# A selective scan laid out over (state, channel of a group of eight) in place of one state at a time

## The chip, the cores and the metric

The kernel runs on one core of one Trainium2 chip. A core has five engines that each work through a queue of their own, in order: TensorE (PE, matrix products into PSUM), VectorE (DVE, elementwise work, reductions, scans), ScalarE (ACT, functions such as exp, copies), GpSimd (POOL, elementwise work on SBUF) and SyncE (SP, issues transfers). Time is microseconds of device time for the whole program. The kernel before took 25469.25 us, the median of three runs (25460.89, 25469.25 and 25479.85).

## The reference

The input is eight images of 64 channels and 64 x 64 positions. Four layers follow one another: attention over all positions with a depthwise block (layer 0), two blocks of attention in windows with an MLP (layer 1), filters made from the data with a 1 x 9 convolution (layer 2), and a selective scan in four directions followed by a small multi-scale block (layer 3). The change touches the scan of layer 3. Cut to that, for one image, 128 channels, 16 states, four directions k and 4096 positions in the order of the direction:

```python
x_dbl = einsum('bkdl,kcd->bkcl', xs, xproj_w)          # 4 + 16 + 16 rows
dts, Bs, Cs = split(x_dbl, [4, 20], axis=2)
dts = softplus(einsum('bkrl,kdr->bkdl', dts, dtproj_w) + dtproj_b)
A = -exp(A_logs).reshape(4, 128, 16)
def step(h, inp):                                       # over the 4096 positions
    u_t, dt_t, B_t, C_t = inp
    h = h * exp(dt_t[..., None] * A) + dt_t[..., None] * B_t[:, :, None, :] * u_t[..., None]
    return (h, einsum('bkcn,bkn->bkc', h, C_t))         # sum over the 16 states
```

So for every position there are 128 x 16 running states; each needs a decay factor exp(dt * A), an input dt * u * B, one step of the recurrence, and a product with C that is summed over the states. The four directions are added.

## The kernel before, in words

The images are handled in pairs; a tile's partitions are (image, channel). Layers 0 to 2 work on a pair. Layer 3 runs `ss2d` once for each image of the pair, with the 128 scan channels on the partitions, so there are eight scan stages in a run. Everything else of the program (layers 0 to 2, the norms, `safm`) is the same before and after the change but for one number, the slots of the pool of large tiles.

A scan stage goes through 16 units of work: four directions (0, 2, 1, 3), each cut into four pieces of `TC` = 1024 positions. For a piece, `scan_inputs` (from L777) makes what the scan needs: a matmul with 36 output rows (`px`, L787) gives B, C and the low-rank part of dt; the 32 rows of B and C are written to memory (`rows`, issued by ACT); a second matmul (`pd`, L803), absolute value, exp and log (L808 to L812) and two VectorE operations (L810, L813) give dt, and one more (L814) gives dt * u. These inputs are made for the piece after the one being scanned (`ahead`).

`scan` (from L819) then loops over the 16 states, partition = channel:

- `bc` (L842): a transfer of 1 MB, issued by SP, that copies the state's rows of B and C onto all 128 partitions.
- `da` (L844): ACT computes exp(dt * A[:, n]) with the state's column of A as the scale.
- `v` (L846): VectorE multiplies dt * u with B.
- `h` (L849): VectorE's scan instruction runs the recurrence along 1024 positions, from a carried column.
- `carry` (L852): ACT copies the last column out.
- `v` (L853): VectorE multiplies h with C.
- `y` (L837): PE adds v into PSUM with an identity matrix, two matmuls of 512 columns; it accumulates over the 16 states.

At the end VectorE adds y to the output `Y` (L861 or L863). Pools have two buffers for each name unless a number stands with them, so a step can run at most two states ahead of what consumes it. A scheduler fixes the order of instructions on each engine when the program is built; it places an instruction by the program's order and by when a buffer is free, and nothing is reordered when it runs.

## Time and profile before

| what | us |
| --- | --- |
| median of three runs | 25469.25 |
| the profiled execution, first to last instruction (its span) | 25403.5 |
| PE busy in it | 19006.6 |
| VectorE busy | 16255.3 |
| ScalarE busy | 6244.3 |
| GpSimd busy | 654.9 |
| the eight scan stages, first `px` to last addition to `Y` | 1408.4 to 1414.0 each |

The profile times every instruction of one execution. "Busy" is the time in which an engine had an instruction under way. A matmul of fp32 data appears as two records, each with a weight load of its own. In a group's line the count, the busy time, the mean of one instruction in ns, and the idle time of the engine ahead of the group are given, with what ended that idle time. PEclk is the share of TensorE's clock that was granted.

### The profile page before, as it was taken

To read this page: it belongs to the slowest core of one execution; us is meant where nothing else is said; L and a number is where in the kernel's file an instruction comes from. 1 tells how busy PE (TensorE), PEld (TensorE's weight loads), DVE (VectorE), ACT (ScalarE), POOL (GpSimd) and SP (SyncE) were. 2 spreads that over 40 slices of the span, in tenths; PEclk is the share of its full clock that TensorE was granted. 3 is DMA by queue.
4 is the path that set the end of the run, shared out by engine and by line. 5 is a ranking of instruction groups with operands and counts; after the bars stand their busy time and mean duration, and the time that the engine had idled before them with its cause. 6 is when DMAs were issued, how large, how long until landed. Compare 5 with 4: busy or idle time off the path is not lost.

```text
span 25403.5 us, 118768 instructions
## 1 busy us (share of the span) xinstructions
PE 19006.6 (75%) x41752; PEld 7027.5 (28%) x41752; DVE 16255.3 (64%) x13458; ACT 6244.3 (25%) x8413; POOL 654.9 (3%) x817
## 2 busy tenths in 40 slices
PE   9998855565999885555599888555659988856565
PEld 4433311111443331111144333111114433311111
DVE  2225589898222558989822255898982225589898
ACT  0123232232012323223201232322320123232232
POOL 0001000000000100000000010000000001000000
PEclk9787777777678777777767877777766787777776
DMA  0000045454000005545400000554540000055453
GB/s 14 2 0 1 1 170 193 155 195 144 7 2 0 1 1 172 194 156 195 142 5 2 0 1 1 176 193 154 195 142 5 2 0 1 1 176 193 156 196 136
DMA packets 570550, 2209.23 MB, mean 87 GB/s; under 512 B 35680, under 2 KB 35680, under 8 KB 568288
## 3 DMA queue, kind: packets, MB, share of 16 engines
q1 hardware_dynamic: 563520, 2181.17, 24.9%
q10 hardware_dynamic: 6432, 20.47, 0.3%
q8 instruction: 329, 5.39, 0.1%
q14 instruction: 269, 2.20, 0.0%
HBM read 2176.33 MB, written 25.17 MB: 87 GB/s over the span
## 4 chain that ended last, share of the span: by engine, by line
PE 47%; DVE 32%; DMA 17%; ACT 3%; issue 2%; DVEq 0%; ACTq 0%; POOL 0%
DMA bc<-rows 17%; PE s L366 14%; DVE h L849 11%; PE s L397 7%; PE po L390 7%; DVE v L846 5%; DVE v L853 5%; PE ws L510 3%; DVE n_sd L313 3%; PE av L546 2%; PE n_v L310 2%; PE pb L678 2%; PE pt L538 1%; PE py L690 1%; PE wpv L524 1%
## 5 line engine op out<-in xcount | busy, mean ns | idle before, releaser
L837 PE MATMUL y<-v,pack 128*128 128x512 f32 x8192 | 6098.2, 887 | 4265.7 <-DVE v L853 4265.7
L837 PEld LDWEIGHTS y<-v,pack 128*128 128x128 f32 x8192 | 1926.1, 259 | 8458.3 <-DVE v L853 6521.2
L849 DVE TENSOR_TENSOR_SCAN h<-da,carry,v 128x1024 f32<-128x1024 f32 x1536 | 3609.7, 2350 | 144.6 <-DVE v L846 4.6
L366 PE MATMUL s<-X 64*128 64x512 f32 x4096 | 3498.5, 1057 | 10.6 <-DMA X<-in_x 10.6
L844 ACT ACTIVATE da<-dt,A 128x1024 f32<-128x1024 f32 x2048 | 2327.8, 1137 | 1880.4 <-DVE h L849 1878.8
L846 DVE TENSOR_TENSOR v<-dtu,bc 128x1024 f32<-128x1024 f32 x2048 | 2503.5, 1222 | 433.6 <-DMA bc<-rows 411.8
L369 DVE TENSOR_REDUCE mx<-s 128x1 f32<-128x1024 f32 x1024 | 1253.5, 1224 | 2310.8 <-PE s L366 2310.8
L853 DVE TENSOR_TENSOR v<-h,bc 128x1024 f32<-128x1024 f32 x2048 | 2506.6, 1224 | 61.8
L407 DVE RECIPROCAL rec<-po 64x512 f32<-64x512 f32 x64 | 214.7, 3355 | 3378.1 <-PE po L390 3378.1
L366 PEld LDWEIGHTS s<-X 64*128 64x128 f32 x4096 | 1365.5, 334 | 2130.4 <-issue 2118.3
L397 PE MATMUL s<-RQ,QK 65*128 65x512 f32 x4096 | 1924.2, 593 | 0.0
L390 PE MATMUL po<-e,VT 128*128 128x512 f32 x4096 | 1917.8, 592 | 0.0
L852 ACT ACTIVATE carry<-h 128x1 f32<-128x1 f32 x1536 | 311.5, 203 | 5562.4 <-DVE h L849 5555.6
L401 ACT ACTIVATE e<-s 128x1024 f32<-128x1024 f32 x1024 | 1047.7, 1023 | 2441.8 <-PE s L397 2441.8
L313 DVE RECIPROCAL n_sd<-n_sd 128x512 f32<-128x512 f32 x288 | 963.1, 3348 | 588.1 <-ACT n_sd L312 588.1
L849 DVE TENSOR_TENSOR_SCAN h<-da,v 128x1024 f32<-128x1024 f32 x512 | 1172.9, 2291 | 46.7 <-DVE v L846 1.8
L510 PE MATMUL ws<-kx,Q 64*64 64x512 f32 x2048 | 1083.5, 722 | 8.4 <-DVE we L513 6.1
L390 PEld LDWEIGHTS po<-e,VT 128*128 128x128 f32 x4096 | 774.3, 189 | 982.5 <-issue 948.3
L397 PEld LDWEIGHTS s<-RQ,QK 65*128 65x128 f32 x4096 | 773.4, 189 | 976.5 <-issue 976.5
L379 ACT ACTIVATE RQ<-pm 1x512 f32<-1x512 f32 x64 | 37.6, 587 | 3550.2 <-PE pm L376 3549.9
L310 PE MATMUL n_v<-n_sq,pack 128*128 128x512 f32 x576 | 503.7, 971 | 428.5 <-DVE H L321 255.8
L787 PE MATMUL px<-XC,pack 128*36 128x512 f32 x512 | 424.6, 970 | 530.8 <-ACT XC L733 334.6
(207 smaller groups left out, 14412.4 us busy)
## 6 DMA issues: line engine op xcount, KB each, us to landing
bc<-rows SPq DMA_DIRECT2D x2048, 1024.0 KB, 5.2
rows<-xd ACTq DMA_DIRECT2D x128, 128.0 KB, 2.1
X<-in_x SPq DMA_DIRECT2D x4, 2048.0 KB, 10.3
QK<-in_x SPq DMA_DIRECT2D x8, 1024.0 KB, 7.2
RQ<-in_x SPq DMA_DIRECT2D x8, 1024.0 KB, 7.2
out<-Y SPq DMA_DIRECT2D x32, 256.0 KB, 2.0
pack<-in_w ACTq DMA_DIRECT2D x1, 3169.0 KB, 29.4
pack<-in_w ACTq DMA_DIRECT2D x1, 424.5 KB, 10.0
```

Source lines behind the costliest of these rows:

```text
L313: nc.vector.reciprocal(sd, sd)
L366: nc.tensor.matmul(s[:, h, :], lhsT=X[lo, t * P : (t + 1) * P], rhs=X[lo, o : o + CH], start=True, stop=True)
L369: nc.vector.tensor_reduce(mx[:, t, q : q + 1], s, AX.XY, ALU.max)
L390: nc.tensor.matmul(po, lhsT=VT[:, t, :], rhs=e[:, h, :], start=(t == 0), stop=(t == 31))
L397: nc.tensor.matmul(s[:, h, :], lhsT=QK[0:65, t * P : (t + 1) * P], rhs=RQ[0:65, cols], start=True, stop=True)
L401: nc.scalar.activation(e, s, AF.Exp, scale=C**-0.5)
L510: nc.tensor.matmul(s[lo], lhsT=Q[lo, cols], rhs=kx[lo], start=True, stop=True)
L837: nc.tensor.matmul(y[:, hc], lhsT=w["ident"], rhs=v[:, hc], start=(n == 0), stop=(n == NST - 1))
L844: nc.scalar.activation(da, dt, AF.Exp, scale=self.A[:, k, n : n + 1])
L846: nc.vector.tensor_tensor(v, dtu, bc[:, 0, :], ALU.mult)
L849: nc.vector.tensor_tensor_scan(along(h), along(da), along(v), first, ALU.mult, ALU.add)
L853: nc.vector.tensor_tensor(v, h, bc[:, 1, :], ALU.mult)
```

## The change

The scan is laid out anew. `TC` goes from 1024 to 512, so a stage has 32 pieces in place of 16. A step `u` of the inner loop no longer covers one state of 128 channels; it covers all 16 states of a group of eight channels, partition = state * 8 + channel. There are again 16 steps a piece. `r` is the strip of 32 channels that the group lies in, `q` its place in the strip.

- Decay: PE multiplies dt (the 32 channels of a strip, so 32 rows of contraction) with `asel`, a table that picks the eight channels and carries A; the product goes to PSUM (`da`, three buffers) and ACT applies exp in place there.
- Input: dt * u is written to memory (`rows`), and one transfer of 1 MB for each four steps (`ub`) brings each channel's row to its 16 partitions. B comes from a matmul whose weights repeat each state's row eight times (`BB`). GpSimd multiplies `ub` with `BB` into `v` (four buffers).
- Scan: VectorE, 512 columns, decay from PSUM and input from SBUF, result in `h` (three buffers).
- Product with C: on even steps GpSimd multiplies h with `CC` (SBUF), on odd steps VectorE multiplies h with `pc3` (the same values, made by one more matmul and kept in PSUM). Both write into `v`.
- Sum over states: PE multiplies v with `ysel`, which adds the 16 states of each of the eight channels into the strip's 32 rows of `y`; 128 rows of contraction, 32 output rows.
- `scan_inputs`: the low-rank product for dt is folded into one matrix beforehand (`xdt`), so one matmul gives `pd`; two more give `BB` and `CC`.
- The pool of large tiles has five slots in place of six, and the tables `asel` and `xdt` are made once at the start. The packed weights are larger.

Comments in the file went too; they are left out here.

```diff
-TC = 1024
+GD = P // NST
+TC = 512
 ...
-    put("xpT", np.concatenate([xp[:, RNK:], xp[:, :RNK]], axis=1).transpose(2, 0, 1))
 ...
+    put("xbT", np.repeat(xp[:, RNK : RNK + NST], GD, axis=1).transpose(2, 0, 1))
+    put("xcT", np.repeat(xp[:, RNK + NST :], GD, axis=1).transpose(2, 0, 1))
+    put("xr", xp[:, :RNK].transpose(1, 0, 2))
+    put("dtT", f["dtproj_w"].transpose(2, 0, 1))
+    e32 = np.eye(32, dtype=np.float32)
+    put("gsel", np.concatenate([e32] * 4, axis=0).reshape(P, 4, GD))
+    put("ysel", np.concatenate([e32.reshape(4, GD, 32)] * NST, axis=1).transpose(1, 0, 2))
 ...
-        self.slabs = ctx.enter_context(tc.tile_pool(name="slabs", bufs=6))
+        self.slabs = ctx.enter_context(tc.tile_pool(name="slabs", bufs=5))
 ...
+        self.asel = const.tile([P, KDIR, 4, NST * GD], F32, name="asel", tag="asel")
+        for k in range(KDIR):
+            for q in range(4):
+                nc.vector.tensor_tensor(
+                    self.asel[:, k, q].rearrange("p (n d) -> p n d", d=GD),
+                    A[:, k, :].unsqueeze(2).to_broadcast([P, NST, GD]),
+                    w["gsel"][:, q, :].unsqueeze(1).to_broadcast([P, NST, GD]),
+                    ALU.mult,
+                )
 ...
+            pd = ps.tile([P, CH], F32, name="pd", tag="pr", bufs=2)
+            nc.tensor.matmul(pd, lhsT=self.xdt[:, k, :], rhs=xc[:, h * nr : (h + 1) * nr, :], start=True, stop=True)
 ...
-        return rows, dt, dtu
+        rows = self.dram.tile([32, 4, TC], F32, name="rows", tag="rows")
+        nc.scalar.dma_start(rows.rearrange("m r t -> r m t"), dtu)
+        for to, wt in ((BB, "xbT"), (CC, "xcT")):
+            for h in range(TC // CH):
+                pb = ps.tile([P, CH], F32, name="pb3", tag="pr", bufs=2)
+                nc.tensor.matmul(pb, lhsT=w[wt][:, k, :], rhs=xc[:, h * nr : (h + 1) * nr, :], start=True, stop=True)
+                nc.scalar.activation(to[:, h * CH : (h + 1) * CH], pb, AF.Copy)
+        return rows, dt, BB, CC
 ...
+        pc = ps.tile([P, TC], F32, name="pc3", tag="pc", bufs=1)
 ...
+        for u in range(NST):
+            q, r = u // 4, u % 4
+            g = 4 * r + q
+            rs = slice(32 * r, 32 * r + 32)
+            if r == 0:
+                ubs = wk.tile([P, 4, TC], F32, name="ub", tag="ub")
+                nc.sync.dma_start(
+                    ubs.rearrange("p r t -> p (r t)"),
+                    rows[GD * q : GD * q + GD].rearrange("d r t -> d (r t)").unsqueeze(0).to_broadcast([NST, GD, 4 * TC]),
+                )
+            ub = ubs[:, r, :]
+            da = ps.tile([P, TC], F32, name="da", tag="da", bufs=3)
             for h in range(TC // CH):
                 hc = slice(h * CH, (h + 1) * CH)
-                nc.tensor.matmul(y[:, hc], lhsT=w["ident"], rhs=v[:, hc], start=(n == 0), stop=(n == NST - 1))
+                nc.tensor.matmul(da[:, hc], lhsT=self.asel[rs, k, q, :], rhs=dt[rs, hc], start=True, stop=True)
+            nc.scalar.activation(da, da, AF.Exp)
+            v = wk.tile([P, TC], F32, name="v", tag="v", bufs=4)
+            nc.gpsimd.tensor_tensor(v, ub, BB, ALU.mult)
+            h3 = wk.tile([P, TC], F32, name="h", tag="h", bufs=3)
+            first = 0.0 if at == 0 else self.carry[:, g : g + 1]
+            nc.vector.tensor_tensor_scan(along(h3), along(da), along(v), first, ALU.mult, ALU.add)
             if at < NTC - 1:
 ...
+            if u % 2:
+                nc.vector.tensor_tensor(v, h3, pc, ALU.mult)
+            else:
+                nc.gpsimd.tensor_tensor(v, h3, CC, ALU.mult)
+            for h in range(TC // CH):
+                hc = slice(h * CH, (h + 1) * CH)
+                nc.tensor.matmul(y[rs, hc], lhsT=w["ysel"][:, q, :], rhs=v[:, hc], start=(q == 0), stop=(q == 3))
+            if u == NST // 2:
                 following = ahead()
```

## The prediction

> **What bounds the kernel now.** I read the page's busy times and chain, then the windows of the scan stages, then the groups of the scan's lines, and last the rows elsewhere that resemble what the change adds.

> ```profile
> 3248.00:4657.00 1409.00, 839.44 (x1153) 256.86 (x1153) 1300.47 (x832) 423.22 (x546) 0.00 (x0) 0.75 0.56 192
> 4773.00:6185.00 1412.00, 848.56 (x1152) 261.81 (x1152) 1300.07 (x832) 422.80 (x546) 0.67 (x12) 0.74 0.56 193
> ```

> These are two scan stages: length, busy PE, weight loads, VectorE, ScalarE, GpSimd, granted PE clock, DMA share. VectorE works 1300 of 1409 us, GpSimd nothing. The eight stages are 11296 us by their first and last instructions, 44% of the span. Cut to pieces of 512 columns, as the change has them, a stage is 32 x 43.3 us and about 25 us at its ends, and VectorE's work is 40.6 us a piece.

> ```profile
> L849 DVE TENSOR_TENSOR_SCAN h<-da,carry,v 128x1024 f32<-128x1024 f32 x1536 | 3609.7, 2350 | 144.6 <-DVE v L846 4.6
> L846 DVE TENSOR_TENSOR v<-dtu,bc 128x1024 f32<-128x1024 f32 x2048 | 2503.5, 1222 | 433.6 <-DMA bc<-rows 411.8
> L853 DVE TENSOR_TENSOR v<-h,bc 128x1024 f32<-128x1024 f32 x2048 | 2506.6, 1224 | 61.8
> ```

> A step is 1222 + 2350 + 1224 ns of VectorE in a row, with little idle time, and what there is waits for the transfer of B and C. So the stage is worth what VectorE is relieved of, as long as no other engine takes its place.

> **The change part by part**, for a piece of 512 columns; there are 256.

> VectorE. Two rows at 512 and 1024 columns (681 ns at L683, 1224 at L853) leave a fixed part of 2 x 681 - 1224 = 138 ns. A scan of 512 is then (2350 + 138) / 2 = 1.25 us; bounds 1.18 (half) and 1.31 (two fixed parts). 16 scans are 20.0 us, 8 products with C at 0.68 are 5.4, `pd` 0.75 (L724 at 512), the softplus sum 0.68, dt * u (1565 + 138) / 2 = 0.85, the addition to Y (1965 + 138) / 2 = 1.05. Together 28.7 us against 40.6.

> GpSimd. The nearest row is a product of the same shape:

> ```profile
> L501 POOL TENSOR_TENSOR kx<-K,pack x512: 1037/1045/1167, 1988.3 to 21810.8; 128x512 f32<-128x512 f32 x171
> ```

> (min, median, max in ns.) 16 inputs and 8 products with C are 24 x 1.045 = 25.1 us, below VectorE's 28.7. [...]

> Do the two engines hinder each other?

> ```profile
> L516 DVE TENSOR_TENSOR we<-we,wmx x512: 678/692/1367, 2007.8 to 21824.2; 128x512 f32<-128x512 f32 x171
> ```

> ```profile
> L513 DVE TENSOR_TENSOR we<-ws,wbias x256: 631/680/693, 2487.7 to 21822.3; 128x512 f32<-128x512 f32 x128
> ```

> L516 reads two SBUF tensors and is stretched up to twice; matching times, those beside a `kx` average 844 ns, the others 687. L513 has one operand in PSUM: 680 beside a `kx`, 676 without. The new scans read decay from PSUM and the odd products C from PSUM, so I take no cost for them; the bound is 24 x 0.16 = 3.8 us a piece.

> ScalarE. 16 exps at 0.60 (L540, 128x512 from PSUM), 14 copies of 0.20, five more of 0.6 to 0.69, two table loads of 1.28: about 18 us. It doesn't bound.

> DMA. Four transfers of 1 MB a piece; the same size lands in 5.2 us (`bc`). The program's order gives each at least six GpSimd instructions, 6.3 us, after its buffer comes free, and `rows` is written a whole piece ahead. Cost nothing; if that cover went, up to 4 x 5.2 = 21 us a piece would show.

> PE. 36 matmuls of 512 columns a piece (16 decay, 16 sums, `pd`, `BB`, `CC`, `pc3`), two records each. A record takes 0.43 us at full clock and 0.86 at half, so 31.0 us or 61.6. This is the part to fear:

> ```profile
> 1000.00:1300.00 300.00, 300.00 (x353) 117.12 (x352) 107.35 (x89) 0.00 (x0) 0.00 (x0) 0.50 0.00 0
> 1500.00:1690.00 190.00, 190.00 (x444) 83.75 (x443) 12.15 (x6) 57.03 (x56) 0.00 (x0) 1.00 0.00 0
> ```

> Both windows of layer 0 have PE busy throughout. The first has only matmuls of 64 rows of contraction (L366) and stays at clock 0.50; the second has 65 and 128 rows and gets 1.00. The clock records change on a grid of 3.41 us. I summed, for each step of the grid, PE's streaming time weighted with rows / 128 (rounded up to 32). At half clock, a step under 0.70 was followed by full clock in 1% of 2598 cases, over 0.78 in 96% of 824. At full clock, a step under 0.39 kept it in 1% of 942, over 0.47 in 99% of 2122. Output columns didn't matter.

> The decay matmuls have 32 rows (weight 0.25), the sums 128. At full clock a piece streams 20 x 0.86 + 16 x 0.86 x 0.25 = 20.6 us, 0.59 of 35 us: it keeps the clock. At half clock and busy throughout, the mean is 24 / 36 = 0.67, too little, but the order has runs of 128-row matmuls (sums 5 and 6, `BB` or `CC`, sum 7; sum 11 with `pd`) that fill a step, so it returns within a piece. [...]

> Matmuls in different row strips overlap:

> ```profile
> 2389.68 1.44 PE L599 MATMUL ph<-H,pack 64*128 64x512 f32 x4
> ```

> Four records, partly at half clock, in 1.44 us. Where two decays or two sums stand together and are ready, they share a slot; the order has 27 slots for 36. A decay and a sum can't share.

> **Stalls.** I walked the order of one piece through the four queues. (a) Exp 9 stands behind the state copy of scan 8 on ScalarE: scan 9 starts 0.20 + 0.60 + 0.1 = 0.9 us late. (b) The table loads ahead of the next piece's first exp: 0.5. (c) `v` has four buffers; inputs 12 and 14 stand on GpSimd right behind products 8 and 10 and need their sums done first, so GpSimd idles 1.2 us twice (a sum takes 1.07 us to its end), and scans 13 to 15 wait: 1.3. (d) PE, 31.0 us of work in about 31, queues up, and a lapse of the clock for one step delays two matmuls by 0.86 each; from 0 (pairs, no lapse) up to a PE bound at half clock; I take two lapses a piece, 3.5 us, since 0.59 lies nearer to the full clock's rows. Total 28.7 + 0.9 + 0.5 + 1.3 + 3.5 = 34.9 us.

> Elsewhere: tables at the start and the larger weights, about 20 us, ahead of the first reductions on VectorE. The fifth slot: outside the scan the order is the same to a few instructions, and the tiles freed late are awaited by loads that 447 us of L366 cover. Nothing.

> **Sum.** 8 x (32 x 34.9 + 25) = 9134 against 11296: -2162, +20. The profiled execution is 25403.5; the median lies 65.75 above, and I keep that: 25469.25 - 2142 = 23327, say 23330.

> **The rivals.**
> 1. The clock stays low (the other side). For it: L366, 447 us at half clock, and the stage's mean of 0.75 now. Against: the 128-row runs. Then 27 to 36 slots at 1.71 us are 46.2 to 61.6 us a piece: 26200 to 30100. It decides above 43.3 us a piece, a mean slot of 1.20 us over 36.
> 2. GpSimd paces. Each even product waits for its scan (1.25) and the next input for the sum (1.2): with six of eight exposed 25.1 + 6 x 2.45 = 39.8 us, with eight 44.7; from 38 to 44.7 it gives 24100 to 25850, mostly still faster. For it: one queue with both kinds of work. Against: the order has two to four inputs ahead of most products.
> 3. VectorE and GpSimd block each other after all: 34.9 + 3.8 = 38.7 us, 24300; a full block of each of 24 by 0.69 gives 51.5, 27600. L513 speaks against it.

> **How the numbers follow.** Forecast 0.56, rival 1 0.16, rival 2 0.20, rival 3 0.08. Its own range is 22150 (scans at 1.18 us, term d at 0) to 24100 (38 us a piece). The range for 8 in 10 takes in rival 2 but for its end: 22150 to 25600, leaving out rival 1's 0.14, half of rival 3 and 0.02 below. Faster: 0.56 + 0.15 + 0.02 + 0.03 = 0.76; slower 0.22; same 0.02. Within 0.2% is about what a measurement can't tell from no change.

> **What would show it.** A stage of about 1140 us; VectorE's scans near 1250 ns and GpSimd's products near 1045; VectorE busy for 80% of the stage; PEclk above 0.8 in it; few idle times that end on `ub`. A clock near 0.5, GpSimd products well above 1.1 us, or scans above 1.35 would make it wrong.

## The result, and the profile after

The changed kernel takes 26564.39 us, the median of four runs (26408.26 to 26647.20), against 25466.50 for the kernel before in the same session (four runs, 25460.89 to 25479.85). The ratio is 1.0424, with a 95% interval of 1.0391 to 1.0456. The forecast was 23330 us and a range up to 25600, so the sign is wrong. The kernel before took 25426, 25426 and 25411 us in the three later sessions, so a difference between two sessions can be off by some 50 us. The profiled execution has a span of 26572.2 us.

A stage, from its first scan to its last, takes 1501 to 1547 us, where about 1140 was forecast, some 25 us at the ends included. Cut to pieces of 512 columns, the mean is 47.7 us against the forecast's 34.9: 256 pieces x 12.8 us = 3277 us, and the time is 3234 us above the forecast. Outside the stages (first input matmul to last addition to `Y`) the profiled execution takes 14133 us, against 14107 before: the miss lies in the scan stages.

Two windows, which lie in the first and the second scan stage of the kernel after. The columns are as in the prediction: length, busy PE, weight loads, VectorE, ScalarE, GpSimd, granted PE clock, DMA share, GB/s.

```profile
3290.00:4820.00 1530.00, 1412.01 (x2284) 278.91 (x2284) 913.44 (x891) 510.86 (x1173) 986.50 (x772) 0.66 0.41 94
4950.00:6480.00 1530.00, 1399.99 (x2286) 278.10 (x2286) 918.25 (x892) 510.05 (x1173) 985.44 (x784) 0.67 0.41 94
```

VectorE has been relieved as planned: 913 us of 1530, 60%, where it was 92%. GpSimd has 64%. PE is busy for 92% at a clock of 0.66: it is the bound now, and as its clock records hold only 1.00 and 0.50, a mean of 0.66 is half clock for 68% of the time.

The groups of the scan's lines, from the page of the kernel after (busy us, mean ns of one, idle time before and what ended most of it), with the row from elsewhere that priced GpSimd:

```profile
L881 POOL TENSOR_TENSOR v<-ub,BB 128x512 f32<-128x512 f32 x4096 | 5379.1, 1325 | 5385.4 <-PE y L894 3781.0
L884 DVE TENSOR_TENSOR_SCAN h<-da,carry,v 128x512 f32<-128x512 f32 x3584 | 4517.0, 1277 | 3358.1 <-ACT da L879 1551.6
L894 PE MATMUL y<-v,pack 128*32 128x512 f32 x8192 | 4988.0, 879 | 853.4 <-POOL v L891 645.0
L878 PE MATMUL da<-dt,asel 32*128 32x512 f32 x8192 | 4915.7, 915 | 80.6 <-DVE h L884 80.6
L879 ACT ACTIVATE da<-da 128x512 f32<-128x512 f32 x4096 | 2329.7, 581 | 5939.0 <-PE da L878 5911.5
...
L891 POOL TENSOR_TENSOR v<-h,CC 128x512 f32<-128x512 f32 x2048 | 2585.8, 1269 | 177.8 <-DVE h L884 177.1
L524 POOL TENSOR_TENSOR kx<-K,pack 128x512 f32<-128x512 f32 x512 | 535.6, 1050 | 6238.1 <-DVE K L515 3246.0
...
L889 DVE TENSOR_TENSOR v<-h,pc 128x512 f32<-128x512 f32 x2048 | 1385.0, 676 | 96.7 <-PE pc L855 11.6
```

Read the right-hand ends as a circle. The scan's idle time ends most often with the exp (L879, 1551.6 of 3358.1 us); the exp idles for 5911.5 us until PE has made `da`; GpSimd idles for 3781.0 us until PE's sum `y` frees a `v`; and PE's own 853.4 us of idle time ahead of `y` end mostly with GpSimd's product (L891). Most waits lead to PE, and where PE itself waits, it is mostly for GpSimd.

How the clock falls is seen in PE's timeline of the kernel after (start, duration, idle time before with what ended it). Between 3347.33 and 3378.05 us the clock is full, and then it is half for 58.03 us:

```profile
3360.24 1.13 PE L878 MATMUL da<-dt,asel 32*128 32x512 f32 x4
3361.30 1.05 PE L894 MATMUL y<-v,pack 128*32 128x512 f32 x2
3362.28 1.13 PE L816 MATMUL pd<-XC,xdt 128*128 128x512 f32 x2
3363.33 1.12 PE L878 MATMUL da<-dt,asel 32*128 32x512 f32 x2
3365.39 1.05 PE L894 MATMUL y<-v,pack 128*32 128x512 f32 x4 [0.94 <-POOL v L891]
3366.62 1.05 PE L894 MATMUL y<-v,pack 128*32 128x512 f32 x2 [0.18 <-POOL v L891]
3367.60 1.13 PE L878 MATMUL da<-dt,asel 32*128 32x512 f32 x6
3368.66 1.05 PE L894 MATMUL y<-v,pack 128*32 128x512 f32 x2
3370.78 1.12 PE L878 MATMUL da<-dt,asel 32*128 32x512 f32 x2 [1.07 <-DVE h L884]
3372.12 1.67 PE L894 MATMUL y<-v,pack 128*32 128x512 f32 x4 [0.22 <-POOL v L891]
3373.72 1.34 PE L878 MATMUL da<-dt,asel 32*128 32x512 f32 x4
3376.95 1.04 PE L894 MATMUL y<-v,pack 128*32 128x512 f32 x2 [1.89 <-POOL v L891]
3377.93 1.98 PE L878 MATMUL da<-dt,asel 32*128 32x512 f32 x2
3379.84 1.92 PE L894 MATMUL y<-v,pack 128*32 128x512 f32 x2
3381.68 2.08 PE L855 MATMUL pc<-XC,pack 128*128 128x512 f32 x2
3383.69 2.07 PE L878 MATMUL da<-dt,asel 32*128 32x512 f32 x2
3385.69 1.92 PE L894 MATMUL y<-v,pack 128*32 128x512 f32 x2
```

Three things are to be seen (`x2` is one matmul, that is two records). At full clock PE has gaps, and four of the five here end on GpSimd's product L891. Two or three decays (`x4`, `x6`), or two sums, that stand together mostly ran at once in the time of one (1.05 to 1.13 us; two pairs here took 1.34 and 1.67). After the gap of 1.89 us every matmul takes about 2 us, PE has no gaps any more, and in the lines shown it does one matmul at a time.

The prediction's measure, PE's streaming time weighted with the rows of contraction, can be taken on the 3.41 us grid of this trace (all but the last of its 1068 clock records last a whole multiple of 3.413 us; the two named above last 30.72 and 58.03, 9 and 17 of them), with matmuls that run at once counted once. (From here on a "step" is a step of this grid, where the loop isn't named.) The step that begins at 3374.64 holds 0.28; the next is at half clock. The 16 steps from there hold 0.50 to 0.69; the seventeenth holds 0.89, and after it the clock is full again. Counting neighbours once fits better here: counted twice, four of the 16 steps would hold 1.04 to 1.18, where over 0.78 was followed by full clock in 96% of cases in the kernel before, and the clock stayed at half. In all the stages 362 steps at half clock hold under 0.70 counted once and over 1.0 counted twice; 315 of them were followed by half clock.

### The profile page after: what moved, and what is told of

Same layout as the page of the kernel before. It is cut to its first block, busy times and chain, and to the rows that moved or that the text cites. A ratio compares the mean times of both kernels' runs of the same rounds, so it can differ in the third digit from the quotient of the medians.

```text
span 26572.2 us, 151496 instructions
## 1 busy us (share of the span) xinstructions
PE 23680.7 (89%) x50976; PEld 7240.7 (27%) x50976; DVE 13216.0 (50%) x13986; ACT 7024.5 (26%) x13534; POOL 8539.1 (32%) x6961
## 5 line engine op out<-in xcount | busy, mean ns | idle before, releaser
L881 POOL TENSOR_TENSOR v<-ub,BB 128x512 f32<-128x512 f32 x4096 | 5379.1, 1325 | 5385.4 <-PE y L894 3781.0
L884 DVE TENSOR_TENSOR_SCAN h<-da,carry,v 128x512 f32<-128x512 f32 x3584 | 4517.0, 1277 | 3358.1 <-ACT da L879 1551.6
L894 PE MATMUL y<-v,pack 128*32 128x512 f32 x8192 | 4988.0, 879 | 853.4 <-POOL v L891 645.0
L878 PE MATMUL da<-dt,asel 32*128 32x512 f32 x8192 | 4915.7, 915 | 80.6 <-DVE h L884 80.6
L879 ACT ACTIVATE da<-da 128x512 f32<-128x512 f32 x4096 | 2329.7, 581 | 5939.0 <-PE da L878 5911.5
L891 POOL TENSOR_TENSOR v<-h,CC 128x512 f32<-128x512 f32 x2048 | 2585.8, 1269 | 177.8 <-DVE h L884 177.1
L524 POOL TENSOR_TENSOR kx<-K,pack 128x512 f32<-128x512 f32 x512 | 535.6, 1050 | 6238.1 <-DVE K L515 3246.0
L878 PEld LDWEIGHTS da<-dt,asel 32*128 32x128 f32 x8192 | 1272.6, 255 | 3953.8 <-issue 2273.2
L894 PEld LDWEIGHTS y<-v,pack 128*32 128x32 f32 x8192 | 536.9, 127 | 4775.2 <-POOL v L891 1859.0
L889 DVE TENSOR_TENSOR v<-h,pc 128x512 f32<-128x512 f32 x2048 | 1385.0, 676 | 96.7 <-PE pc L855 11.6
```

Source lines behind the costliest of these rows:

```text
L878: nc.tensor.matmul(da[:, hc], lhsT=self.asel[rs, k, q, :], rhs=dt[rs, hc], start=True, stop=True)
L879: nc.scalar.activation(da, da, AF.Exp)
L881: nc.gpsimd.tensor_tensor(v, ub, BB, ALU.mult)
L884: nc.vector.tensor_tensor_scan(along(h3), along(da), along(v), first, ALU.mult, ALU.add)
L889: nc.vector.tensor_tensor(v, h3, pc, ALU.mult)
L891: nc.gpsimd.tensor_tensor(v, h3, CC, ALU.mult)
```

## The experiments

The times are medians of four runs and more, but for one run that is named. Theory 1 was that PE's clock alone, held down by the 32-row decays, makes the time; theory 2 that GpSimd with its 1.27 us products does. In the short diffs the line that is changed is shown, not its surroundings.

**Decays over 128 rows.** The table is padded with zeros, so the matmul streams all of dt and computes the same. Order and number of PE's, ScalarE's and GpSimd's instructions stay as they are. (One table serves all four directions, which have equal `A_logs` in this input.)

```diff
-    nc.tensor.matmul(da[:, hc], lhsT=self.asel[rs, k, q, :], rhs=dt[rs, hc], start=True, stop=True)
+    nc.tensor.matmul(da[:, hc], lhsT=self.asel[:, 0, u, :], rhs=dt[:, hc], start=True, stop=True)
```

> Edit: the changed kernel with the decay matmul run over all 128 rows of dt, against a table that is zero outside the strip (the table of direction 0 serves all four directions, as A_logs has the same values in each). The same 36 matmuls a piece, the same work on every other engine; pairs of decays can no longer overlap. Theory 1 (the clock: 32-row decays keep TensorE's row-weighted time too low, the clock falls to half and PE sets the pace): clock in the scan stages above 0.95, a piece 36 to 38 us in place of 47.7, total 23800 to 24200. Theory 2 (GpSimd: its products cost 1266 ns where 1045 were reckoned, and its queue of 24 with round trips over the sums sets the pace): GpSimd's work is untouched, a piece stays above 45, total 26000 or more.

Measured: 23796.51 us, a ratio to the kernel before of 0.9363 [0.9349, 0.9377], with a piece of 37.0 us; 3 us below theory 1's range. The same view of two of its stages:

```profile
3300.00:4460.00 1160.00, 1082.52 (x2252) 266.12 (x2252) 896.45 (x876) 508.38 (x1153) 969.61 (x759) 1.00 0.52 121
4650.00:5800.00 1150.00, 1072.90 (x2227) 262.80 (x2226) 888.59 (x865) 503.64 (x1134) 955.67 (x758) 1.00 0.51 119
```

and its timeline of PE:

```profile
3365.89 1.05 PE L897 MATMUL y<-v,pack 128*32 128x512 f32 x2 [0.72 <-POOL v L894]
3366.87 1.13 PE L881 MATMUL da<-dt,asel 128*128 128x512 f32 x2
3367.93 1.05 PE L897 MATMUL y<-v,pack 128*32 128x512 f32 x4
3368.91 1.98 PE L881 MATMUL da<-dt,asel 128*128 128x512 f32 x4
```

The matmuls carry four times the rows, two decays no longer run at once (1.98 us for `x4`, where the 32-row form took 1.13), PE still waits for GpSimd, and yet the kernel is 2768 us faster, at a clock of 1.00 where it was 0.66. Here rows without any use for the result brought the clock: of 2724 full-clock steps in the stages, 2 are under 0.39, where it was 431 of 1103.

The padding changes two things, the rows and the sharing of slots, so it must be asked which of them holds the clock. The steps tell: with the decays counted at 32 rows, 534 of the full-clock steps would hold under 0.39, while with 128 they hold over 0.47. All 534 kept the clock; of the changed kernel's steps under 0.39, 18% did. So in this run the rows of zeros counted.

**All products with C on VectorE**, decays with 32 rows as in the changed kernel. GpSimd is left with the 16 inputs of a piece.

```diff
-    if u % 2:
+    if True:
         nc.vector.tensor_tensor(v, h3, pc, ALU.mult)
```

> Edit: the changed kernel with all 16 products with C on VectorE, against C in PSUM; GpSimd keeps the 16 inputs. Theory 1 (clock): PE's work and its rows are the same, so 26200 to 26800, clock in the stages 0.62 to 0.70. Theory 2 (GpSimd): its work falls from 30.4 to 20.3 us a piece, up to 10 us a piece or 2590 us in all: 24000 to 24800.

Measured: 24637.10 us, ratio 0.9692 [0.9676, 0.9709], 40.4 us a piece. Theory 1's number missed and theory 2's hit; but the gain comes with a higher clock:

```profile
3290.00:4500.00 1210.00, 1176.57 (x2102) 251.26 (x2102) 942.67 (x1053) 478.06 (x1091) 607.47 (x470) 0.74 0.47 108
4700.00:5950.00 1250.00, 1177.63 (x2190) 254.58 (x2191) 987.64 (x1093) 511.81 (x1147) 625.82 (x489) 0.78 0.48 110
```

PE is busy for 94 to 97% of these windows, more than in the changed kernel, and it is still the bound. So neither theory stands alone: GpSimd's lateness seems to act on the clock. Moving the products also gave PE, VectorE and ScalarE a new order, so the gain isn't GpSimd's relief alone.

**Both edits together.**

> Edit: both of the two before, decays over 128 rows and all products with C on VectorE. Theory 1: the clock is high, and VectorE has about 34.5 us of work a piece and stalls on top: 37 to 39 us, 24000 to 24400, no better than the decays over 128 rows alone. Theory 2: as all products on VectorE, 24000 to 24800, and no better than that edit alone.

Measured: 23911.91 us, ratio 0.9408 [0.9394, 0.9422], 37.5 us a piece at a clock of 0.99; just under theory 1's range and no better than the padding alone, as it said. The order is that of the kernel with all products with C on VectorE. Taking the eight products a piece from GpSimd to VectorE is worth 1927 us with 32-row decays and costs 115 us with 128-row ones. GpSimd now waits for the transfer `ub` within the stages too: between 3300 and 4460 us 25 times, 125.0 us in all and up to 6.9 at once, where the kernel with 128-row decays alone has no such wait. How much of the 115 us that is stays open.

**A cheaper product on GpSimd.** The input product reads a single column of B, broadcast along the row (it leaves out that B depends on the position). No engine's order changes.

```diff
-    nc.gpsimd.tensor_tensor(v, ub, BB, ALU.mult)
+    nc.gpsimd.tensor_tensor(v, ub, BB[:, 0:1].to_broadcast([P, TC]), ALU.mult)
```

> Edit: the changed kernel with GpSimd's input product reading one column of B, broadcast along the 512 columns, in place of 512 values of B (so B's dependence on the position is left out). If a broadcast operand is what makes the earlier product in layer 1 take 1045 ns, v comes to about 1045 ns and the even products with C stay at 1266. If work of the other engines beside it makes it longer, both stay at 1266. The total: theory 1 within 1.5% of the changed kernel; theory 2 lower by up to 256 x 3.5 = 900 us.

Measured, in one run: 25209.44 us, 42.3 us a piece. It is 1355 us below the changed kernel, more than either theory said, and the clock in the pieces rises from 0.67 to 0.77. The line's instructions (min/median/max ns) in the changed kernel, with the row `kx` that priced them in the prediction:

```profile
L881 POOL TENSOR_TENSOR v<-ub,BB x4096: 1252/1266/2141, 3303.2 to 26376.7; 128x512 f32<-128x512 f32 x196
```

```profile
L524 POOL TENSOR_TENSOR kx<-K,pack x512: 1037/1045/1167, 2013.0 to 22692.7; 128x512 f32<-128x512 f32 x171
```

and in the kernel with the broadcast operand:

```profile
L881 POOL TENSOR_TENSOR v<-ub,BB x4096: 1029/1040/2003, 3296.9 to 25012.2; 128x512 f32<-128x512 f32 x196
```

The rows have one shape, but `kx` reads a broadcast operand, which the printed shape hides. The dense product took 1266 ns, the two with a broadcast operand 1040 and 1045.

**The same with 128-row decays**, again with no engine's order changed, to see what GpSimd is worth when the clock is full:

> The kernel with 128-row decays, and GpSimd's input product reads one column of B, broadcast along the row (the kernel leaves out that B depends on the position). 16 of the 24 products of a piece then take some 1.10 us in place of 1.27, which makes GpSimd's work 27.8 us in place of 30.4. Theory A (GpSimd's own time is on the path at full clock): 34 to 35.5 us a piece, 23050 to 23400 us. Theory B (it isn't; VectorE with its hand-overs or PE sets the pace): 23650 to 23850.

Measured: 23610.06 us, ratio 0.9286 [0.9272, 0.9300], 36.1 us a piece. It lies just below theory B's range: 186 us less than with the dense product, or 0.84 us a piece for 3.6 us taken from GpSimd (the mean of its 16 inputs falls from 1328 to 1101 ns; 2.7 us had been expected). The two edits to GpSimd and the two forms of the decay, in us:

| | 32-row decays | 128-row decays |
| --- | --- | --- |
| GpSimd as in the change | 26564 | 23797 |
| input product with a broadcast operand | 25209 | 23610 |
| all products with C on VectorE | 24637 | 23912 |

Across a row every engine's order is the same but for the decay's form; the third row has another order than the first two, and eight more products a piece on VectorE. The cheaper product is worth 1355 us in the left column and 186 in the right, the moved ones 1927 and -115. In these runs nearly all that a late GpSimd cost went with the clock; the cheaper product shows it cleanly, with one run in the left column.

**Decays over 64 rows**, the dose in between (each direction has its own table; order unchanged).

```diff
-    lhsT=self.asel[rs, k, q, :], rhs=dt[rs, hc]
+    lhsT=self.asel[rs64, k, 2 * q + r % 2, :], rhs=dt[rs64, hc]     # rs64: the 64 rows that hold the strip
```

> The decay matmul runs over 64 rows of contraction in place of 32, the added rows holding zeros; all four directions keep their own tables. Everything else is the changed kernel. This is the dose between the changed kernel and the one with 128 rows (23796.5 us, 37.0 us a piece). Row-weighted PE work of a piece is then 20 x 0.86 + 16 x 0.86 x 0.5 = 24.1 us at full clock, and 48.2 of 61.6 us, a mean of 0.78, at half clock with PE busy throughout. Theory A (the clock returns where the row-weighted activity of a 3.41 us step passes about 0.74, as in the trace of before): 0.78 lies above it, so the clock always returns; 23700 to 24000 us, 37 us a piece, clock in the stage above 0.95. Theory B (the clock follows the weight gradually, so half of the dose brings about half of the gain): 24800 to 25700 us, clock 0.75 to 0.9. Theory C (the 128-row run gained by something else than the weight, such as matmuls that no longer overlap in different row strips): above 25700.

Measured: 24120.17 us, ratio 0.9485 [0.9467, 0.9502]; the clock in the pieces is 0.94. Half the dose brings 2444 of the 2768 us, 88%, so theories B and C fall. Theory A's range is missed by 120 us: 177 of 248 pieces have a full clock and take 37.0 us, but once lost the clock is away for 16.2 us on average. Some pairs of 64-row decays still run at once (1467 of 8192 records start within 0.4 us of the one before, 2373 in the changed kernel and none with 128 rows), so the steps at half clock hold 0.67 and not the 0.78 of the expectation.

**More buffers for v and h** (six and four in place of four and three) on the 128-row kernel.

> The kernel with 128-row decays, with six buffers for v in place of four and four for h in place of three. Theory A (at full clock the rest of the piece, 37.0 us against VectorE's 28.7, is stalls of the v buffers and of GpSimd's round trip, term c of the prediction and more): 33 to 35 us a piece, 22800 to 23300 us. Theory B (at full clock PE's in-order queue or GpSimd's own work of 24 x 1.27 = 30.4 us sets the pace, and buffers don't matter): 23700 to 23900.

Measured: 24217.85 us, ratio 0.9524 [0.9510, 0.9538]: slower by 421 us than without, which no theory said. The scheduler places instructions by free buffers and wrote another order for all engines, so this run doesn't test the stall on `v` buffers. It shows only that such a kernel with another order can cost 1.6 us a piece more.

**Two of eight products with C moved to VectorE**, first with those buffers, then without them.

```diff
-    if u % 2:
+    if u % 2 or u % 8 == 4:
```

> The kernel with 128-row decays and six v and four h buffers, and two of the eight even products with C of a piece (states u = 4 and 12) move from GpSimd to VectorE: GpSimd has 22 products, 27.9 us, VectorE about 30.2 us of work. Theory A (GpSimd paces, and two round trips are gone): 300 to 800 us below the kernel with the added buffers alone. Theory B (VectorE or PE paces): within 100 us of it, or up to 350 us above.

> The kernel with 128-row decays and each direction's own table, and two of GpSimd's eight products with C of a piece (states u = 4 and 12) on VectorE; buffers as in the changed kernel. Theory A (a us taken from GpSimd shortens a piece by 0.3 us, as the 2.7 us of the broadcast run did by 0.84): 2 x 1.27 x 0.3 = 0.8 us a piece, 23550 to 23700. Theory B (VectorE's two added products, 1.36 us, cost what they relieve, as the run with all products on VectorE suggests, 23912 us): 23800 to 24000.

Measured: 23872.05 us, 346 less than its counterpart with the same buffers and so in theory A's range; and 24062.17, 173 more than its counterpart (the next kernel) and 62 above theory B's range. The signs differ, and both have a new order on every engine. What the shift itself is worth at full clock isn't settled by these runs.

**A complete kernel with 128-row decays.** Each direction has its own table, whose blocks VectorE rewrites ahead of the direction.

```diff
+    for j in range(16):
+        js = slice(32 * (j % 4), 32 * (j % 4) + 32)
+        nc.vector.tensor_tensor(self.asel[js, j]..., self.A[js, k, :]..., w["gsel"][js, j // 4, :]..., ALU.mult)
```

> The 128-row decays with each direction's own table: one zero-padded table, whose diagonal blocks VectorE writes anew ahead of each direction (16 products of 32x128 a stage). A complete kernel. If the extra VectorE work costs what it takes, some 16 x 0.2 us in each of 8 stages, 25 us: 23790 to 23880 us. If the wait of a stage's first decay for its table drains PE's queue, some 10 us more in each stage: up to 23950.

Measured: 23888.69 us, ratio 0.9393 [0.9378, 0.9409]; 8.7 us above the first range, within the second. The 0.2 us of the expectation was an estimate of the author; the nearest row, the table's products of 128x128 in the changed kernel, has a median of 285 ns. The kernel needs nothing of the input's tables and beats both kernels: the one before by 6.1%, the changed one by 9.9% (0.9393 / 1.0424 = 0.901).

**Less work for PE at full clock.** Every fourth decay factor is made by ScalarE straight from dt, in one instruction as before (leaves out the right decay factors of 4 of the 16 steps of a piece).

```diff
+    if u % 4 == 3:
+        nc.scalar.activation(da, dt, AF.Exp, scale=-1.0)
```

> The 128-row kernel, and every fourth decay is not a matmul: ScalarE computes exp(-dt) straight from dt, one instruction as before (leaves out the right decay factors of 4 states of 16). PE has 32 matmuls a piece in place of 36, 4 x 0.86 = 3.4 us less; VectorE, GpSimd and ScalarE have the same work. Theory A (at full clock PE with its in-order queue sets the pace, busy 34.5 of 37.0 us a piece): 33 to 35 us a piece, 22750 to 23300 us. Theory B (GpSimd, VectorE and their hand-overs set it): 36 to 37.5 us, 23550 to 23950.

Measured: 23541.88 us, ratio 0.9266 [0.9251, 0.9282]; 36.0 us a piece, between the theories and 8 us under B's range. The mean mixes two cases. 115 of 248 pieces keep the full clock and take 34.3 us, in theory A's range: 2.7 us less for 3.4 us less of PE. The others lose the clock for a step and take 37.7 (eight more at 34.4 aside); where 128-row matmuls are taken away, 151 steps fall under 0.39 again. The order is a new one here too, so this speaks for PE as the pace at full clock but doesn't settle it.

**The kernel before with five slots for its large tiles.**

```diff
-    self.slabs = ctx.enter_context(tc.tile_pool(name="slabs", bufs=6))
+    self.slabs = ctx.enter_context(tc.tile_pool(name="slabs", bufs=5))
```

> The kernel before with five buffers of its slab pool in place of six, nothing else: the part of the change that the prediction costed at nothing. Theory A (the loads that wait for a slab are covered by work of the next layer 0): within 0.2% of the kernel before. Theory B (the missing slab makes a load or the next stage late): 100 us or more slower, 25 us for each of four images at least.

Measured: 25371.56 us, ratio 0.9985 [0.9976, 0.9994]. The fifth slot costs nothing, as predicted; it may even help by 40 us.

## Why the prediction was wrong, point by point

**What bounds the kernel before** was right, and so was VectorE's relief. The scan of 512 has a median of 1282 ns (1.25 forecast, bounds 1.18 and 1.31), the products with C on VectorE a mean of 676 (0.68), the exp of 581 (0.60), and VectorE's work is 913 us of a 1530 us window, 0.597 x 47.7 = 28.5 us a piece (28.7 forecast).

**GpSimd's price** was mis-sized: 24 x 1.045 = 25.1 us rested on a row with a broadcast operand. Dense it is 24 x 1.266 = 30.4, above VectorE's 28.7. Against VectorE's product with C that is 1266 / 676 = 1.87, where the prediction's rows, 1045 and 681 ns, stand at 1.53. As work GpSimd is still hidden (64% busy). It cost where the prediction had put nothing at all: it makes even sums late, and these sit in PE's queue ahead of decays.

**Rival 3**, mutual blocking, did not happen between product and scan: GpSimd's product has a median of 1266 ns beside no scan and 1265 to 1270 ns beside scans. Only the 776 inputs beside the two VectorE instructions with two SBUF operands (L821, L822) were stretched, to 1574 ns on average: 0.9 us a piece.

**The clock** is the step that failed. It had two halves, "0.59 of 35 us: it keeps the clock" and "the order has runs of 128-row matmuls ... that fill a step, so it returns within a piece".

The first took a mean over a piece, where the clock records change from one step of 3.41 us to the next. In the stages of the changed kernel 1103 steps are at full clock. With matmuls that run at once counted once, they hold 0.45 on average, not 0.59, with a standard deviation of 0.15; 431 of them, 39%, are under 0.39, and 82% of these are followed by half clock. The mean is lower because a waiting PE streams nothing (at full clock in the stages PE is busy for 82% of the time) and because neighbours that share a slot, which the prediction counted as a saving of time, are counted once (counted twice the mean is 0.55). The spread is put down to decays next to each other and to waits for L891, as in the timeline above.

The second half overlooked the same sharing: sums 5 and 6 do stand together, but in different strips they ran in one slot of 1.9 us, not in two, and fill no step. At half clock 2433 steps hold 0.60 on average; 291, or 12%, pass 0.78. Where no two run at once, PE's order alternates a decay (0.25) with a sum (1.0), whose mean of 0.62 is below 0.70; of the half-clock steps under 0.70, 2% in the kernel before and 3% here were followed by full clock. So the state held itself in this run: at half clock PE is the bound, is busy for 98% of the time, and still 82% of the steps are under 0.70.

**Term (d)** in numbers: two lapses of the clock a piece were taken, each of one step of 3.4 us, 3.5 us of delay in all. There were 358 lapses in 256 pieces, 1.4 a piece, of 22.5 us on average, while spells at full clock last 10.5 us. So the number of lapses was fair, and the length was too short by a factor of 6.6.

**The rest of the walk** was short too, by less. The four pieces that the changed kernel ran at a clock of 0.9 or more took 34.7 to 35.8 us from first scan to first scan, 35.5 on average; the 128-row kernel takes 37.0. That 34.9 was forecast is close to this by luck, since 3.5 of it were meant for lapses: without them the walk comes to 31.4 us. So of the 12.8 us by which a piece was missed, an estimated 8.7 (47.7 - 35.5 - 3.5) are the clock beyond term (d), and 4.1 (35.5 - 31.4) are GpSimd's dense product, its stretching and waiting in queues. How these 4.1 divide stays open; at full clock the cheaper product took 0.84 us off a piece. The transfers cost nothing, as forecast: between 3320 and 4460 us GpSimd waits for `ub` once, for 1.1 us.

**The rivals' weights.** Rival 1, "the clock stays low", had the mechanism, the price (46.2 to 61.6 us a piece, 26200 to 30100 us) and the chance of 0.16. What the prediction set against it was the 128-row runs, the very point that fell. Rivals 1 and 2 were also weighed as if independent: a late GpSimd takes work from PE's steps, so what makes rival 2 likely makes rival 1 likely. The bounds 0.39, 0.47, 0.70 and 0.78 are counts of steps in the kernel before; how the chip sets its clock no run shows. There neighbours counted once or twice make hardly a difference (counted once, a step under 0.70 regained the clock in 2% of cases and one over 0.78 in all 716), so its trace couldn't tell which count holds. (Output columns: all 255 of its full-clock steps over 0.47 whose work is mostly that of matmuls with 64 columns or fewer kept the clock.) In the changed kernel's stages all 556 full-clock steps over 0.47 kept the clock, and 88% of the half-clock steps over 0.78 regained it; at the lower end it is less sharp: steps under 0.39 kept the clock in 18% of cases, where it had been 1%. In the kernels with the broadcast operand and with 64 rows it was 44% and 65%, so 0.39, or the way in which neighbours are counted, isn't exact.

**The gap that lost the clock** in the timeline above lasted 1.89 us, in a step with a pair of 32-row decays. Two such decays, in different strips, ran at once in 1.13 us, where two with 128 rows took 1.98; yet it was the form with 128 rows, one after the other, that was faster by 2768 us.

## What to carry to other kernels

Where PE gets matmuls with few rows of contraction, take from the kernel's own trace PE's work weighted with rows for every step of the grid on which the clock records change (3.41 us here), neighbours that ran at once counted once and waits as zeros, and look at the lowest steps, not at the mean. In the stages of the changed kernel the full clock was kept after all steps over 0.47 and after 18% of those under 0.39. Where a trace shows the same, padding the contraction with zeros to 128 rows is worth trying first; here it took off 2768 us. A matmul that ran alone cost no more PE time so (1.12 us with 32 rows, 1.13 with 128, both at full clock); neighbours that ran at once did (1.13 us for two, then 1.98). When a duration is taken from another line, compare the operands' access patterns and not only the printed shapes.

## What the runs showed of the hardware that was not expected

```profile
PEclk9787666666668766666666886666666687667666
```

```profile
PEclk9787789999678778999967877899996787789999
```

- In the changed kernel, matmuls that ran at once are better counted once: 315 of 362 steps at half clock that hold under 0.70 so, and over 1.0 with neighbours counted twice, were followed by half clock.
- The dose was not linear: 64 rows brought 2444 of the 2768 us, 88%.
- A product of two dense 128x512 fp32 tensors took GpSimd 1266 ns in the changed kernel, and 1040 with one operand broadcast along the row (medians).
- Some 0.2 us more in 16 of GpSimd's 24 products of a piece cost 1355 us (one run) with 32-row decays, at a clock of 0.67 in the pieces, and 186 us with 128-row ones, at 1.00.
